# Channel mix in float32r over coefficients stored in two parts, and column transforms in full precision beside it

## The chip, the cores and the metric

The kernel runs on one core of a Trainium2 chip. The metric is the device time of one execution in microseconds (us). The engines are TensorE (PE in the profile, with its weight loads shown apart as PEld), VectorE (DVE), ScalarE (ACT), GpSimd (POOL) and SyncE (SP). [...]

## The reference

The input x has 4 images of 64 channels, each 256 x 256, in float32. Four layers follow one another. Layers 0, 1 and 3 are the same kind: per channel, a two-dimensional causal convolution with a filter that is an outer product, plus a bias times the input. Layer 2 is a Haar transform with channel mixing and soft thresholding:

```python
k = jnp.einsum('ijk,imk->ijmk', hx, hy)[0]          # layers 0, 1, 3
y = irfft2(rfft2(x) * rfft2(k) / fft_size)[..., :L, :L]
out = y + x * bias[:, None, None]
...
f1 = haar2d(x)                                       # layer 2
for i in range(2):
    f3 = f1 * v[i]
    f4 = jnp.einsum('bchw,oc->bohw', f3, conv_w[i])
    acc = acc + jnp.sign(f4) * jax.nn.relu(jnp.abs(f4) - tau[i])
y = haar2d(acc, inverse=True) + x
```

## The kernel before

**The products.** As the filters are outer products, a convolution becomes two products with Toeplitz matrices (`contract`, lines 248 and 249), in full float32: data are the stationary operand (128 x 128), a Toeplitz tile `t` of 256 or 128 columns is the moving one. A full-precision product shows as two weight loads and two matmul records. Each product's result `pa` is copied out of PSUM by ScalarE (line 262); each second result `py` gets the bias term on VectorE (line 279).

**The stages.** One image passes three stages. *Convolutions* (`convolutions`): layers 0 and 1 channel by channel, then the row part of the Haar transform on VectorE (`pairs`, `levels`, in the ring of eight tiles `sd`), then the column part on TensorE (`down`), whose result `pz` is copied by ScalarE to `co` and stored in the DRAM tensor `coef` (`away`). *Mixing* (`mixing`): 64 groups of four coefficient rows, loaded with channels on the partitions, mixed over channels on TensorE (`mix`), scaled, thresholded and added into the resident tile `z`. *Inverse* (`inverse`): channel by channel back, then layer 3. While image b is mixed and inverted, the convolutions of image b + 1 are laid between; beside the last image's mixing stand the layer-3 convolutions of a third of the channels, which had been put off to `late`.

**The column transform.** In `down` every channel is split into two float32r parts, a rounded copy (`split`, line 337, ScalarE) and the difference (`rest`, line 342, VectorE), and two products of 512 columns with the same stationary matrix `hbr` add up in PSUM. A full-precision branch with `hbt` is in the code; no channel takes it, since `in_parts` holds all of them.

**The mix.** A group's tile `f` has 128 partitions: two coefficient rows (k) by 64 channels. Slices of 128 columns are the stationary operand, and `wb`, in which the 128 x 256 matrix has the mixing weights twice on its diagonal and zeros beside, is the moving one. Four full-precision products of 256 columns make one group.

**The order.** [...] `at(time, run, unit)` collects every step with a due time in ticks, `PLACE` holds the fraction of a tick of each kind of step, and the steps are issued in the order of these times. A tick is one channel or one group. On VectorE the order in the trace departs from the due times in places, where a step's input comes later; on TensorE and ScalarE it follows them. `after` stretches the ticks of the last eight channels past `border`, the start of the inverse stage. SyncE issues nearly all loads and stores in this order, ScalarE the outputs and `late`.

**Buffers.** PSUM has four banks (`psm`) for convolutions and transforms and two double banks (`psx`) for the mix. The pool `toep` has five Toeplitz tiles; tag "in" has three tiles for loaded images; tag "f" has three, shared by the mix's loads and the inverse's `r`; tag "co" has two.

## Time and profile before

| | |
|---|---|
| time, median of 3 runs | 2973.84 us (2973.59 to 2974.6) |
| span of the profiled execution, first to last instruction | 2971.0 us |
| granted TensorE clock | 1.0 throughout |
| first convolutions, alone | until about 453 us |
| mixing stages of the four images (first to last mix product) | 453 to 858, 1088 to 1529, 1763 to 2204, 2433 to 2706 us |
| last inverse stage | from 2723 us to the end |
| moved by DMA | 649.7 MB, 219 GB/s on average |
| busy share of the 16 DMA engines | 0.76 between 30 and 420 us, 0.69 to 0.81 later |

The profiled execution's span is given; the times of the three runs are measured apart from it and lie 2.6 to 3.6 us above it. In the profile's groups, a line reads: line of the code, engine, operation, tiles written and read, shapes, count, then busy time and the mean length of one instruction, then the engine's idle time just before and what ended it. Records of matmuls overlap, since they are pipelined; the distance between their starts tells what one costs.

### The profile page before, as it was taken

Reading aid. Unit: us, or ns where it says so; the run is one execution under the profiler, and the core shown is the slowest. Engines: PE = TensorE matmul, PEld = TensorE weight load, DVE = VectorE, ACT = ScalarE, POOL = GpSimd, SP = SyncE. Lnnn points to the kernel's source line nnn. Section 1 sums busy time; section 2 is a strip of 40 time slices with the busy share of each in tenths; the row PEclk is TensorE's granted clock in tenths of the full one; section 3 lists DMA queues with packets and bytes.
Section 4 is the critical chain, followed back from the end, with each engine's and each line's share of the span. In section 5 each row is a group of like instructions: output and inputs, shape, how many; then the busy total and the mean of one; then the engine's idle time right before and its main releaser. Section 6 shows DMA issues by size and latency. Waiting matters only on the chain. (4 is left out here: it accounts for less than half of the span.)

```text
span 2971.0 us, 52173 instructions
## 1 busy us (share of the span) xinstructions
PE 2905.9 (98%) x16950; PEld 2615.2 (88%) x16950; DVE 2529.6 (85%) x4571; ACT 2183.4 (73%) x5142; POOL 0.2 (0%) x4
## 2 busy tenths in 40 slices
PE   8999999999999999999999999999999999999999
PEld 6899988888888998888888998888888998888998
DVE  5766768999988879999988878999998889998776
ACT  2333338999986768889986768999986768887554
POOL 0000000000000000000000000000000000000000
PEclk9999999999999999999999999999999999999999
DMA  5887777776667876767777876777677888777676
GB/s 156 246 235 230 225 234 213 210 208 195 210 196 238 255 222 199 210 209 208 209 220 229 255 228 199 210 211 211 206 211 231 255 245 235 234 231 220 212 211 186
DMA packets 562498, 649.74 MB, mean 219 GB/s; under 512 B 44369, under 2 KB 447412, under 8 KB 562100
## 3 DMA queue, kind: packets, MB, share of 16 engines
q1 hardware_dynamic: 482996, 562.07, 64.8%
q10 hardware_dynamic: 79232, 84.34, 8.1%
q8 instruction: 137, 2.24, 0.3%
q14 instruction: 133, 1.09, 0.1%
HBM read 426.77 MB, written 219.48 MB: 218 GB/s over the span
## 5 line engine op out<-in xcount | busy, mean ns | idle before, releaser
L248 PE MATMUL py<-t,a 128*128 128x256 f32 x3072 | 920.4, 381 | 11.7 <-ACT a L262 6.3
L262 ACT COPY a<-pa 128x512 f32<-128x512 f32 x768 | 485.8, 633 | 374.7 <-PE pa L249 338.9
L439 ACT ACTIVATE f<-px,vt 128x64 f32<-128x64 f32 x2816 | 619.9, 391 | 113.8 <-DVE f L434 113.2
L249 PEld LDWEIGHTS py<-t,a 128*128 128x128 f32 x3072 | 583.4, 190 | 79.4
L249 PE MATMUL py<-t,a 128*128 128x128 f32 x3072 | 590.0, 274 | 0.0
L248 PEld LDWEIGHTS py<-t,a 128*128 128x128 f32 x3072 | 498.4, 191 | 57.4 <-ACT a L262 18.1
L415 PE MATMUL px<-wb,f 128*128 128x256 f32 x2048 | 486.6, 380 | 6.4 <-ACT f L439 6.4
L415 PEld LDWEIGHTS px<-wb,f 128*128 128x128 f32 x2048 | 369.2, 190 | 48.3 <-ACT f L439 8.5
L248 PE MATMUL pa<-t,y 128*128 128x256 f32 x1024 | 310.0, 385 | 16.7 <-DVE y L279 15.4
L450 DVE TENSOR_TENSOR mag<-mag,vt 128x1024 f32<-128x1024 f32 x256 | 313.3, 1224 | 10.8 <-ACT mag L443 10.2
L443 ACT ACTIVATE mag<-f 128x1024 f32<-128x1024 f32 x256 | 299.8, 1171 | 20.4 <-DVE z L458 19.6
L454 DVE SCALAR_TENSOR_TENSOR mag<-mag,f 128x1024 f32<-128x1024 f32 x256 | 313.3, 1224 | 0.9
L504 ACT CAST w<-pw 128x512 fp32r<-128x512 f32 x256 | 150.3, 587 | 221.6 <-PE pw L496 208.9
L248 PE MATMUL pa<-t,x 128*128 128x256 f32 x1024 | 305.8, 380 | 1.1 <-issue 1.1
L446 ACT ACTIVATE f<-f 128x1024 f32<-128x1024 f32 x256 | 288.1, 1125 | 4.4 <-DVE y L279 1.2
L488 ACT COPY zc<-z 128x512 f32<-128x512 f32 x256 | 282.5, 1104 | 10.9 <-DVE z L289 6.3
L342 DVE TENSOR_TENSOR sp<-sd,sp 128x512 fp32r<-128x512 f32 x256 | 176.5, 689 | 105.0 <-ACT sp L337 103.6
L248 PE MATMUL pa<-t,u 128*128 128x256 f32 x772 | 231.0, 381 | 10.2 <-issue 9.5
L519 DVE SCALAR_TENSOR_TENSOR t<-r,pu 128x512 f32<-128x512 f32 x256 | 175.5, 685 | 65.6 <-PE pu L511 65.0
L279 DVE SCALAR_TENSOR_TENSOR y<-x,bsb,py 128x512 f32<-128x512 f32 x256 | 190.8, 745 | 39.3 <-PE py L249 39.2
L279 DVE SCALAR_TENSOR_TENSOR y<-y,bsb,py 128x512 f32<-128x512 f32 x256 | 190.3, 744 | 38.0 <-PE py L249 37.8
L249 PEld LDWEIGHTS pa<-t,y 128*128 128x128 f32 x1024 | 194.5, 190 | 26.4
(67 smaller groups left out, 4470.8 us busy)
## 6 DMA issues: line engine op xcount, KB each, us to landing
t<-pad SPq DMA_DIRECT2D x768, 256.0 KB, 3.9
x<-in_x SPq DMA_DIRECT2D x256, 256.0 KB, 3.6
keep<-sd SPq DMA_DIRECT2D x256, 256.0 KB, 2.9
coef<-co SPq DMA_DIRECT2D x256, 256.0 KB, 3.1
f<-coef SPq DMA_DIRECT2D x256, 256.0 KB, 3.3
r<-keep SPq DMA_DIRECT2D x256, 256.0 KB, 3.3
out_y<-y ACTq DMA_DIRECT2D x256, 256.0 KB, 4.0
late<-u ACTq DMA_DIRECT2D x63, 256.0 KB, 3.0
```

The source lines that it names most:

```text
L248: nc.tensor.matmul(ps[:, m, :], src[:, 0, m * P : (m + 1) * P], t[:, ::-1], start=True, stop=False)
L249: nc.tensor.matmul(ps[:, m, P:], src[:, 1, m * P : (m + 1) * P], t[:, : P - 1 : -1], start=False, stop=True)
L262: nc.scalar.copy(a, s["p" + new])
L279: nc.vector.scalar_tensor_tensor(y, s[res], bsb[:, layer, c : c + 1], s["p" + new], ALU.mult, ALU.add)
L342: nc.vector.tensor_tensor(w[:, 1], t, w[:, 0].bitcast(F32), ALU.subtract)
L415: nc.tensor.matmul(ps[:, h, q, :], f[:, q, h * P : (h + 1) * P], wb.rearrange("p r n -> p (r n)"), start=True, stop=True,)
L439: nc.scalar.mul(f4[:, j], px[:, j], scale(g, 0)[:, j : j + 1])
L443: nc.scalar.activation(mag, st[g]["f4"], AF.Abs)
L446: nc.scalar.activation(st[g]["f4"], st[g]["f4"], AF.Sign)
L450: nc.vector.tensor_sub(mag, mag, over(g, 1, 16))
L454: nc.vector.scalar_tensor_tensor(mag, mag, 0.0, st[g]["f4"], ALU.max, ALU.mult)
L488: nc.scalar.copy(a, z[:, :, :, c].rearrange("p h (i k) -> p h k i", k=2))
```

## The change

The diff below does the following.

- `coef` gets another layout and twice the size: a float32r rounding of each coefficient (`hi`) and the float32 difference to it (`lo`), each channel's two coefficient rows side by side. `away` writes the rounded copy. A new step `low`, due 0.316 ticks later, subtracts on VectorE and stores the difference; until then the PSUM bank stays in use.
- A group's tile `f` now has the two parts by 64 channels on its 128 partitions and holds 512 KB instead of 256. It has two buffers instead of three, is typed float32r, and is loaded from GpSimd's queue.
- `wb` holds the mixing weights, the same on both halves of the partitions, in two float32r parts. `mix` makes 16 float32r products of 128 columns a group: for each of the eight output slices one with the small part of the weights and one with the large, added up in PSUM.
- `down` takes the full-precision product for channels that fall due before `border`, in other words beside a mixing stage; the others keep the two parts. `split` and `rest` fall away with it. The first image has no border and keeps all its parts.
- The inverse's `r` moves to tag "in".

```diff
+    "low": 1.05,
...
-    wb = const.tile([P, 2, P], F32, name="wb")
+    wb = const.tile([P, 2, P], F32R, name="wb")
...
-    coef = [dram.tile([2, C, P, S], F32, name=f"coef{b}") for b in range(B)]
+    coef = [dram.tile([2, C, P, 2, S], F32, name=f"coef{b}") for b in range(B)]
...
-        nc.vector.memset(wb, 0.0)
         for r in range(2):
-            nc.sync.dma_start(wb[r * C : (r + 1) * C, r, :], wmix)
+            nc.sync.dma_start(mixw[r * C : (r + 1) * C, :], wmix)
+        nc.scalar.copy(wb[:, 0], mixw)
+        nc.vector.tensor_tensor(wb[:, 1], mixw, wb[:, 0].bitcast(F32), ALU.subtract)
...
         def away(c):
-            t = io.tile([P, 2, S], F32, name=f"co_{b}_{c}", tag="co", bufs=BUFS["co"])
-            nc.scalar.copy(t, parts.pop(("ps", c)))
-            nc.sync.dma_start(coef[b][:, c].rearrange("k p w -> p k w"), t)
+            t = parts["hi", c] = mx.tile([P, 2, S], F32R, name=f"hi_{b}_{c}", tag="hi")
+            nc.scalar.copy(t, parts["ps", c])
+            nc.sync.dma_start(coef[b][0, c].rearrange("p k w -> p (k w)"), t.bitcast(F32).rearrange("p k w -> p (k w)"))
+
+        def low(c):
+            t = mx.tile([P, 2, S], F32R, name=f"lo_{b}_{c}", tag="lo", bufs=1)
+            nc.vector.tensor_tensor(t, parts.pop(("ps", c)), parts.pop(("hi", c)).bitcast(F32), ALU.subtract)
+            nc.sync.dma_start(coef[b][1, c].rearrange("p k w -> p (k w)"), t.bitcast(F32).rearrange("p k w -> p (k w)"))
...
-                if c in in_parts:
+                if border is None or end + 4 + j >= border:
+                    in_parts.add(c)
                     at(after(end + 3 + j, n) + PLACE["split"], split, c)
                     at(after(end + 3 + j, n) + PLACE["rest"], rest, c)
...
+                at(after(end + 4 + j, n) + PLACE["low"], low, c)
...
-            f = mx.tile([P, 2, S], F32, name=f"f_{b}_{g}", tag="f", bufs=3)
-            nc.sync.dma_start(f, coef[b].rearrange("k c p w -> (k c) p w")[:, 2 * g : 2 * g + 2])
+            f = mx.tile([P, 2, 2, S], F32R, name=f"f_{b}_{g}", tag="f", bufs=2)
+            nc.gpsimd.dma_start(f, coef[b].rearrange("l c p k w -> (l c) p k w")[:, 2 * g : 2 * g + 2])
...
-            for q in range(2):
-                for h in range(2):
-                    nc.tensor.matmul(
-                        ps[:, h, q, :],
-                        f[:, q, h * P : (h + 1) * P],
-                        wb.rearrange("p r n -> p (r n)"),
-                        start=True,
-                        stop=True,
-                    )
+            for h in range(2):
+                for q in range(2):
+                    for r in range(2):
+                        for i in (1, 0):
+                            nc.tensor.matmul(
+                                ps[:, h, q, r * P : (r + 1) * P],
+                                f[:, q, r, h * P : (h + 1) * P],
+                                wb[:, i],
+                                start=(i == 1),
+                                stop=(i == 0),
+                            )
...
-            r = mx.tile([P, 2, 2, P], F32, name=f"r_{b}_{c}", tag="f", bufs=3)
+            r = io.tile([P, 2, 2, P], F32, name=f"r_{b}_{c}", tag="in", bufs=3)
...
-    nc = _bacc.Bacc("TRN2", target_bir_lowering=False, num_devices=1)
+    nc = _bacc.Bacc("TRN2", target_bir_lowering=False, num_devices=1, dynamic_dma_scratch_size=2048)
```

More of the change, by code (lines that the diff above doesn't have):

```diff
@@ L206, in constants @@
     def constants():
-        signs = part(P)
+        signs, mixw = part(P), part(P)
         nc.sync.dma_start(hbt, haar[0])
@@ L297, in at, with convolutions @@
         events.append((time, len(events), run, unit))
-    def convolutions(b, ticks, in_parts=(), border=None):
+    def convolutions(b, ticks, border=None):
         st = {}
+        in_parts = set()
         def after(tick, n):
@@ L582, in conv_seq_kernel @@
     groups = S // 4
-    ready = convolutions(0, range(C), in_parts=range(C))
+    ready = convolutions(0, range(C))
     ahead = C
@@ L589, in conv_seq_kernel @@
         if b + 1 < B:
-            ready = convolutions(b + 1, spread(ahead, end + 2), in_parts=range(C), border=end)
+            ready = convolutions(b + 1, spread(ahead, end + 2), border=end)
         else:
```

## The prediction

> **What bounds the kernel now.** I read the page's top first: how full each engine is.

> ```profile
> span 2971.0 us, 52173 instructions
> PE 2905.9 (98%) x16950; PEld 2615.2 (88%) x16950; DVE 2529.6 (85%) x4571; ACT 2183.4 (73%) x5142; POOL 0.2 (0%) x4
> ```

> TensorE (PE) is idle for 2971.0 - 2905.9 = 65 us, 14 of them in the first 30 us. An average can hide a stage with another limit, so next the windows by stage: the four mixing stages (columns: length, PE, weight loads, VectorE, ScalarE, GpSimd, clock, DMA share, GB/s).

> ```profile
> 453.00:858.00 405.00, 398.49 (x2179) 350.37 (x2179) 381.86 (x671) 396.73 (x1203) 0.00 (x0) 1.00 0.69 205
> 1088.00:1529.00 441.00, 435.14 (x2440) 391.42 (x2440) 409.39 (x717) 388.21 (x1094) 0.00 (x0) 1.00 0.71 208
> 1763.00:2204.00 441.00, 435.70 (x2441) 391.87 (x2440) 409.67 (x718) 388.70 (x1094) 0.00 (x0) 1.00 0.70 208
> 2433.00:2706.00 273.00, 267.62 (x1454) 239.72 (x1454) 266.13 (x314) 235.87 (x556) 0.00 (x0) 1.00 0.80 234
> ```

> PE is 98% busy in each. In the first, ScalarE is as full (397 of 405); in the last, VectorE (266 of 273). So added PE time lengthens a stage almost one for one, while removed PE time soon meets another engine. The groups that the change touches:

> ```profile
> L415 PE MATMUL px<-wb,f 128*128 128x256 f32 x2048 | 486.6, 380 | 6.4 <-ACT f L439 6.4
> L349 PE MATMUL pz<-sp,hbr 128*128 128x512 f32 x512 | 182.3, 436 | 1.2 <-DVE y L279 0.6 <-DVE sp L342 0.4
> L337 ACT CAST sp<-sd 128x512 fp32r<-128x512 f32 x256 | 184.0, 719 | 3.9 <-DVE sd L328 3.9
> L342 DVE TENSOR_TENSOR sp<-sd,sp 128x512 fp32r<-128x512 f32 x256 | 176.5, 689 | 105.0 <-ACT sp L337 103.6
> L505 DVE TENSOR_TENSOR w<-pw,w 128x512 fp32r<-128x512 f32 x256 | 175.3, 685 | 2.3 <-ACT w L504 2.3
> ```

> Means of pipelined matmuls overlap, so PE prices are distances between starts in the timeline:

> ```profile
> 803.39 0.60 PE L248 MATMUL py<-t,a 128*128 128x256 f32 x2
> 803.83 0.39 PE L249 MATMUL py<-t,a 128*128 128x128 f32 x2
> ```
> ```profile
> 1003.30 0.38 PE L495 MATMUL pw<-hrow,zc 128*128 128x128 f32 x2
> 1003.51 0.27 PE L496 MATMUL pw<-hrow,zc 128*128 128x128 f32 x1
> 1003.62 0.39 PE L495 MATMUL pw<-hrow,zc 128*128 128x128 f32 x2
> ```
> ```profile
> 464.16 0.19 PEld L349 LDWEIGHTS pz<-sp,hbr 128*128 128x128 f32 x1 [0.35 <-DVE sp L342]
> 464.27 0.42 PEld L248 LDWEIGHTS py<-t,a 128*128 128x128 f32 x2
> 464.50 0.59 PE L248 MATMUL py<-t,a 128*128 128x256 f32 x2
> ```

> First fence: a full-precision product over 256 columns (two records) takes 0.43 us, so 0.216 a record. Second: three records of 128 columns take 0.32-0.33 us, about 0.11 each, even the single-record transpose L496. Third, a float32r product whose load had to wait: the next load can start 0.11 after its load, the next product 0.34 after it. So its weight load takes 0.11, and its 512 columns take 0.23. The load is not shorter in float32r.

> [...]

> **The change, part by part.**

> 1. *Mix.* Before: 4 full-precision products of 256 columns a group = 8 x 0.216 = 1.73 us. After: 16 float32r products of 128 columns, each with a weight load of its own (L349 uses one stationary operand twice in a row and still has 512 loads for 512 products, so a repeated one isn't skipped). Streaming 128 columns should take 0.23 / 4 = 0.06, the load 0.11; loads follow one another at 0.11 in the L495/L496 chain. The load sets the pace: 16 x 0.111 = 1.78. Over 256 groups: +0.05 x 256 = **+12 us**. No narrow float32r product is in the trace: bounds are 0.058 (load hidden) and 0.216 [...], which is -205 and +442 us. I take 0.111.

> 2. *Column transforms in full precision.* From the ticks, 54 + 53 + 53 = 160 of 256 channels fall due before the border and get one full-precision product of 512 columns: twice 0.43 = 0.86. The float32r pair takes 0.47 (L249 x2 at 1002.61, L495 at 1003.30: 0.69 less 0.22 for the L249 pair). So +0.39 x 160 = **+63 us** of PE, 21 in each of the first three mixing stages. These channels lose the copy L337 (-0.72 x 160 = -115 us of ScalarE) and the difference L342 (-110 us of VectorE); both hide beside PE.

> 3. *Storing two parts.* The copy out of PSUM stays. New is "low", a subtraction like L505: 0.685 x 256 = +175 us of VectorE, net +65. In mixing, 54 come for 54 gone; in the first convolutions (265 of 390 us busy) 44 us are added. All beside PE. Its wait: it needs ScalarE's copy. Behind it stand add, the y1 sum and the next group's scaling, for which ScalarE's row scaling waits (113 us in all already). But L342 waits for ScalarE alike (103.6 us in 104 waits) and is gone there; VectorE's order in the trace follows readiness, not only due times, so I expect "low" about where L342 was: 0. If it stands ahead of add and y1 sum, the round scaled, ScalarE (2.98 + 0.46 + 0.6), low 0.61, add 0.6, y1 sum 0.66, pairs 0.67, shrink 1.13, scaled 0.3 comes to 8.0 us in the first stage, where PE wants 6.5; with 0.8 channels a group up to +70 us, some +100 over all. The PSUM bank is held some 1.5 us longer; its next user is the fourth bank request after it, some 4 us on: 0. "lo" has one buffer: its transfer (3.1 us for coef) ends well within a tick of 6 to 7 us; where ticks last 3.2 us, about two channels a batch wait some 1 us: 0 to +5.

> 4. *Transfers.* SP loses the group load and gains one store a channel; its stores wait for "low", with toeplitz and x loads behind, some 1.5 us a tick of slack that those loads have (landing 3.6 to 3.9 against 0.93 tick, 5.7 us). The load of 512 KB leaves from GpSimd, whose queue holds nothing else; a buffer comes free when group g-2 is mixed, so it has two groups less one mix: 2 x 4.25 - 1.8 = 6.7 us in the last stage, 11 and more elsewhere. The landing:

> ```profile
> coef<-co SPq DMA_DIRECT2D x256, 256.0 KB, 3.1
> f<-coef SPq DMA_DIRECT2D x256, 256.0 KB, 3.3
> ```

> 3.3 us at 256 KB; [...] It fits. Load on the engines: 134 MB on 650; in the last stage +0.5 us in 4.25, 0.80 to about 0.92 busy; in the first convolutions from 0.76 to 0.87. I allow +5 for slower toeplitz loads.

> 5. *Rest.* r moves from three buffers to three shared with x; only where a last x load falls between the first r loads does one wait, 0.1 us. Splitting the weights (two instructions of 0.3 us) lies beside the first convolutions. ScalarE's 39 us less in each mixing stage may take back over half of the 17.7 us that PE is idle in the three (6.5 + 5.9 + 5.3 in the windows): -10.

> Sum: 2971.0 + 12 + 63 + 5 - 10 + 3 (lo, rest) = 3044 of span. The profiled execution's span lies 2.8 us under the median 2973.84; kept, that gives **3047 us**.

> **The rivals.**
> - *Faster: narrow products hide their load.* [...] At 0.058, 2885, VectorE stopping it. The point is 0.0925 a product: (1.73 - 16t) x 256 = 63. [...] Against: the 0.11 load.
> - *Narrow float32r at the full-precision price.* 0.216 a product: 3.46 a mix, 3047 - 12 + 442 = 3477. Nothing in the trace excludes it[...].
> - *Load and stream don't quite overlap.* A float32r stream takes 0.017 more for its 512 column steps than the 0.216 record; added to each load: 0.128 x 16 = 2.05, about 3117.
> - *The group load is late.* From 6.7 us in the last stage: at 8 us, 1.3 x 64 = +83, 3130.
> - *"low" ahead of its input*, above: up to 3145.
> - *Nothing moves*: t at 0.0925 by chance.

> **How the numbers follow.** Likeliest 59% (3025 to 3075); imperfect overlap 7%, late load 8%, low's wait 7% (3075 to 3150); full price 9%; faster 8%; within 0.2% 2%. Measurement of this kernel tells 0.2% from no change. The range 3010 to 3150 leaves out the full price, the faster case and the unchanged one, 19%. Slower sums to 0.90.

> **What would show it.** Right: mixes start to next product 1.75 to 1.80 us, weight loads 18,998; the transform product 0.86 with 160 + 192 products; mixing stages some 24 us longer, the last some 3; PE still at 98%. Wrong: [...]PE waiting for the group load (step 4), VectorE waiting for the copy with PE idle behind (step 3).

## The result and the profile after

The changed kernel takes 3508.32 us (median of 4 runs, 3503.24 to 3512.85) against 2974.22 us before (4 runs, 2973.59 to 2975.87): 1.179 times as long, 95% interval 1.1777 to 1.181. The prediction was 3047 us in a range of 3010 to 3150. The direction was right; the size missed by 461 us.

The top of the changed kernel's page (busy time, share of the span, instructions):

```profile
span 3503.0 us, 56614 instructions
PE 3139.4 (90%) x18998; PEld 2783.9 (79%) x18998; DVE 2611.7 (75%) x4667; ACT 2110.6 (60%) x4983; POOL 135.6 (4%) x260
```

The weight loads number 18,998, as predicted, but TensorE now idles 3503.0 - 3139.4 = 364 us, where it idled 65. VectorE and ScalarE are emptier too. No engine is full any more. The windows of the four mixing stages (columns as in the prediction):

```profile
473.00:1031.00 558.00, 464.39 (x2687) 402.73 (x2687) 394.78 (x681) 382.40 (x1154) 32.76 (x62) 0.92 0.65 200
1264.00:1831.00 567.00, 496.26 (x2985) 431.46 (x2984) 418.51 (x723) 362.88 (x1047) 32.76 (x62) 0.97 0.71 214
2070.00:2639.00 569.00, 497.32 (x2981) 432.59 (x2980) 418.38 (x724) 363.15 (x1048) 32.77 (x62) 0.97 0.71 213
2874.00:3235.00 361.00, 299.36 (x1965) 276.06 (x1963) 278.91 (x319) 241.14 (x563) 32.76 (x62) 0.94 0.77 221
```

The stages grew from 405, 441, 441 and 273 us to 558, 567, 569 and 361: 495 us of the 532. In each, TensorE idles 62 to 94 us, and its granted clock is 0.92 to 0.97. Even the last stage grew by 88 us, though it holds no column transforms. The transfers are no busier than in the first convolutions before (0.77 between 30 and 450 us). The groups of instructions that the change touches:

```profile
L427 PE MATMUL px<-wb,f 128*128 128x128 f32 x4096 | 530.3, 284 | 3.4 <-ACT mag L455 1.0 <-DMA f<-coef 1.0 <-ACT f L451 0.8
...
L368 DVE TENSOR_TENSOR lo<-pz,hi 128x512 fp32r<-128x512 f32 x256 | 176.0, 688 | 200.6 <-ACT hi L363 163.0 <-DMA coef<-lo 30.7 <-ACT sp L340 6.8
L356 PE MATMUL pz<-sd,hbt 128*128 128x512 f32 x320 | 166.6, 603 | 0.0
...
L352 PE MATMUL pz<-sp,hbr 128*128 128x512 f32 x192 | 68.5, 438 | 0.0
L345 DVE TENSOR_TENSOR sp<-sd,sp 128x512 fp32r<-128x512 f32 x96 | 65.5, 683 | 3.2 <-ACT sp L340 3.0
```

The mix products (L427) wait for almost nothing: 3.4 us in all. 320 records make 160 full-precision transforms (L356), and 192 float32r products remain (L352). Durations between starts, from TensorE's timeline:

```profile
1506.12 1.98 PE L427 MATMUL px<-wb,f 128*128 128x128 f32 x16
1507.93 0.65 PE L250 MATMUL py<-t,a 128*128 128x256 f32 x2
...
1510.61 1.02 PE L356 MATMUL pz<-sd,hbt 128*128 128x512 f32 x2
1511.46 0.59 PE L250 MATMUL py<-t,a 128*128 128x256 f32 x2
```

A mix takes 1.81 us to the next product's start (0.113 a product; 0.111 was predicted), a transform 0.85 (0.86 was predicted). As a record's start shifts with its neighbours (the 256-column product behind this mix has 0.49 us to the next start, 1507.93 to 1508.42, the one behind that 0.43, 1508.64 to 1509.07), a safer measure runs from the start of the product ahead to that of the second product behind. Its medians are 2.38 us around a mix before and 2.44 after (+0.06, where +0.05 was predicted), and 1.12 around a transform in two parts and 1.51 around one in full precision (+0.39, as predicted). The landing times, from the list of DMA issues:

```profile
f<-coef POOLq DMA_DIRECT2D x256, 512.0 KB, 4.6
...
coef<-hi SPq DMA_DIRECT2D x256, 256.0 KB, 3.4
coef<-lo SPq DMA_DIRECT2D x256, 256.0 KB, 2.9
```

4.6 us for the doubled load, where 256 KB took 3.3 before, is below the 6.7 us that step 4 gives it in the last stage. `low` itself takes 0.688 us (0.685 was predicted). So the prices of the products and of the subtraction were met, the mix products wait 1.0 us in all for the load, and most of the time lies elsewhere. The list of waits says where (engine and line, what it waited for: total us, times, longest):

```profile
ACT f L451 <- DVE f L446: 664.9, 250, 7.6
...
DVE mag L462 <- ACT mag L455: 305.2, 136, 3.4
...
PEld pa L250 <- DVE y L281: 196.2, 147, 5.3
DVE lo L368 <- ACT hi L363: 163.0, 93, 3.3
PE pa L250 <- DVE y L281: 152.7, 133, 5.1
```

To read this, the steps of a group: VectorE scales its part of the mix's result (`scaled`) and ScalarE the other rows (row scaling); ScalarE takes the absolute value (Abs) and the sign; VectorE subtracts the threshold (`shrink`), cuts at zero and puts the sign back (`signed`), and adds the result into `z` (`add`). ScalarE's row scaling (L451) waits for VectorE's `scaled` (L446) 665 us; before, the same pair cost 113. VectorE's `shrink` (L462) waits for ScalarE's Abs (L455) 305 us; before 10. Each waits for the other, and TensorE waits for VectorE's y sums (L281). A stretch of VectorE's timeline before (L450 is shrink, L434 scaled, L454 signed, L458 add):

```profile
1297.20 0.42 DVE L434 TENSOR_TENSOR f<-px,vt 128x256 f32<-128x256 f32 x1
...
1303.01 1.22 DVE L450 TENSOR_TENSOR mag<-mag,vt 128x1024 f32<-128x1024 f32 x1
1304.14 0.42 DVE L434 TENSOR_TENSOR f<-px,vt 128x256 f32<-128x256 f32 x1
1304.48 1.22 DVE L454 SCALAR_TENSOR_TENSOR mag<-mag,f 128x1024 f32<-128x1024 f32 x1
1305.61 0.75 DVE L279 SCALAR_TENSOR_TENSOR y<-x,bsb,py 128x512 f32<-128x512 f32 x1
1306.27 0.69 DVE L458 TENSOR_TENSOR z<-mag 128x512 f32<-128x512 f32 x1
```

And after (L462 shrink, L466 signed, L470 add, L446 scaled):

```profile
1515.93 0.69 DVE L368 TENSOR_TENSOR lo<-pz,hi 128x512 fp32r<-128x512 f32 x1 [1.94 <-ACT hi L363]
1516.54 0.74 DVE L281 SCALAR_TENSOR_TENSOR y<-y,bsb,py 128x512 f32<-128x512 f32 x1
1517.19 1.22 DVE L462 TENSOR_TENSOR mag<-mag,vt 128x1024 f32<-128x1024 f32 x1
...
1519.00 1.22 DVE L466 SCALAR_TENSOR_TENSOR mag<-mag,f 128x1024 f32<-128x1024 f32 x1
1520.25 0.69 DVE L470 TENSOR_TENSOR z<-mag 128x512 f32<-128x512 f32 x1
1520.86 0.42 DVE L446 TENSOR_TENSOR f<-px,vt 128x256 f32<-128x256 f32 x1
```

ScalarE's timeline over the same stretch:

```profile
1512.38 2.56 ACT L451 ACTIVATE f<-px,vt 128x64 f32<-128x64 f32 x12 [2.95 <-DVE f L446]
...
1515.69 1.17 ACT L455 ACTIVATE mag<-f 128x1024 f32<-128x1024 f32 x1
...
1521.32 2.56 ACT L451 ACTIVATE f<-px,vt 128x64 f32<-128x64 f32 x12 [2.89 <-DVE f L446]
```

Before, `scaled` of the next group stands between shrink and signed of this one, so ScalarE scales the next group while VectorE finishes this one. After, it stands behind shrink, signed and add. Row scaling, Abs, shrink, signed, add, scaled and the next row scaling then follow one another (in this tick `low` and the y1 sum stand ahead of shrink as well), and a group takes 1521.32 - 1512.38 = 8.94 us instead of 1304.14 - 1297.20 = 6.94 (the distance of two `scaled` before). VectorE's trace keeps the order of its stream: in the first three images `scaled` runs behind signed 63 times of 63, as in the table below. Here L446 runs behind L470, at 1520.86, while ScalarE stands 2.89 us for it.

Nothing in the diff moves `scaled`: its due time and those of the steps beside it are unchanged, and by them `scaled` of the next group comes ahead of shrink (1.583 ticks against 1.777 in the first three images). So the due times alone don't make the order. They feed a scheduler that writes each engine's stream when the kernel is compiled; the experiments below change that order by rules of order alone, and the traces follow them. Counted in VectorE's stream, for the 63 neighbouring groups of each image, `scaled` of g + 1 stands ahead of shrink of g / between shrink and signed / behind signed:

```
                                    image 1     image 2     image 3     image 4
before                              45 18  0     8 50  5     8 50  5    58  4  1
after                                0  0 63     0  0 63     0  0 63     0 27 36
product alone (narrow_only)          0 14 49     0  0 63     0  0 63     0 27 36
transforms alone (down_only)        15 28 20     8  8 47     8  8 47    58  4  1
second copy alone (low_only)        57  6  0    31 27  5    31 27  5    58  4  1
after, 8 products of 256 columns    61  2  0    28 34  1    28 34  1    61  2  0
```

### The profile page after: what moved, and what is told of

Same layout as the page of the kernel before. It is cut to its first block, busy times and chain, and to the rows that moved or that the text cites. A ratio compares the mean times of both kernels' runs of the same rounds, so it can differ in the third digit from the quotient of the medians.

```text
span 3503.0 us, 56614 instructions
## 1 busy us (share of the span) xinstructions
PE 3139.4 (90%) x18998; PEld 2783.9 (79%) x18998; DVE 2611.7 (75%) x4667; ACT 2110.6 (60%) x4983; POOL 135.6 (4%) x260
## 5 line engine op out<-in xcount | busy, mean ns | idle before, releaser
L250 PE MATMUL py<-t,a 128*128 128x256 f32 x3072 | 957.8, 394 | 130.7 <-ACT a L264 126.3
L451 ACT ACTIVATE f<-px,vt 128x64 f32<-128x64 f32 x2816 | 607.0, 345 | 672.8 <-DVE f L446 664.9
L251 PE MATMUL py<-t,a 128*128 128x128 f32 x3072 | 603.5, 279 | 0.0
L462 DVE TENSOR_TENSOR mag<-mag,vt 128x1024 f32<-128x1024 f32 x256 | 313.2, 1223 | 307.5 <-ACT mag L455 305.2
L427 PE MATMUL px<-wb,f 128*128 128x128 f32 x4096 | 530.3, 284 | 3.4 <-ACT mag L455 1.0
L427 PEld LDWEIGHTS px<-wb,f 128*128 128x128 f32 x4096 | 500.7, 199 | 4.8 <-ACT f L451 2.8
L250 PE MATMUL pa<-t,y 128*128 128x256 f32 x1024 | 332.5, 407 | 157.1 <-DVE y L281 151.7
L250 PE MATMUL pa<-t,x 128*128 128x256 f32 x1024 | 327.4, 403 | 43.8 <-DVE lo L368 35.9
L368 DVE TENSOR_TENSOR lo<-pz,hi 128x512 fp32r<-128x512 f32 x256 | 176.0, 688 | 200.6 <-ACT hi L363 163.0
L466 DVE SCALAR_TENSOR_TENSOR mag<-mag,f 128x1024 f32<-128x1024 f32 x256 | 312.7, 1221 | 12.7 <-ACT f L458 7.2
L250 PEld LDWEIGHTS pa<-t,y 128*128 128x128 f32 x1024 | 158.9, 195 | 201.3 <-DVE y L281 194.4
L455 ACT ACTIVATE mag<-f 128x1024 f32<-128x1024 f32 x256 | 292.0, 1141 | 1.7
L458 ACT ACTIVATE f<-f 128x1024 f32<-128x1024 f32 x256 | 281.8, 1101 | 4.3
L407 POOL DMA_DIRECT2D f<-coef x256 | 135.4, 529 | 3087.9 <-PE px L427 2055.5
L330 DVE TENSOR_TENSOR sd<-sd 128x512 f32<-128x512 f32 (+6 forms) x448 | 164.6, 367 | 107.0 <-DMA keep<-sd 57.9
## 6 DMA issues: line engine op xcount, KB each, us to landing
t<-pad SPq DMA_DIRECT2D x768, 256.0 KB, 4.1
x<-in_x SPq DMA_DIRECT2D x256, 256.0 KB, 3.7
keep<-sd SPq DMA_DIRECT2D x256, 256.0 KB, 3.5
coef<-hi SPq DMA_DIRECT2D x256, 256.0 KB, 3.4
coef<-lo SPq DMA_DIRECT2D x256, 256.0 KB, 2.9
r<-keep SPq DMA_DIRECT2D x256, 256.0 KB, 3.5
out_y<-y ACTq DMA_DIRECT2D x256, 256.0 KB, 3.7
```

Source lines behind the costliest of these rows:

```text
L250: nc.tensor.matmul(ps[:, m, :], src[:, 0, m * P : (m + 1) * P], t[:, ::-1], start=True, stop=False)
L251: nc.tensor.matmul(ps[:, m, P:], src[:, 1, m * P : (m + 1) * P], t[:, : P - 1 : -1], start=False, stop=True)
L368: nc.vector.tensor_tensor(t, parts.pop(("ps", c)), parts.pop(("hi", c)).bitcast(F32), ALU.subtract)
L427: nc.tensor.matmul(ps[:, h, q, r * P : (r + 1) * P], f[:, q, r, h * P : (h + 1) * P], wb[:, i], start=(i == 1), stop=(i == 0),)
L451: nc.scalar.mul(f4[:, j], px[:, j], scale(g, 0)[:, j : j + 1])
L455: nc.scalar.activation(mag, st[g]["f4"], AF.Abs)
```

## The experiments

The theory: the work costs about what was predicted, and most of the excess comes from the order on VectorE. The rivals: the narrow products, the new storage or the second copy cost more than their durations show. Ratios are to the kernel before on the same chip, with 95% intervals.

### The order rule on the changed kernel (after_pinned)

```diff
-            nc.vector.tensor_tensor(
+            st["scaled", g] = nc.vector.tensor_tensor(
...
-            nc.vector.tensor_sub(mag, mag, over(g, 1, 16))
+            with tc.issue_after(st["scaled", g + 1].ins):
+                nc.vector.tensor_sub(mag, mag, over(g, 1, 16))
```

> The changed kernel with one ordering rule added and nothing else: on VectorE the subtraction that shrinks group g may not stand ahead of the scaling of group g + 1 (issue order only, no wait). Order theory (the compiler's instruction order on VectorE lost the look-ahead of the scaling, and ScalarE and VectorE take turns): most of the loss goes, 3030 to 3080 us, ScalarE's wait for the scaling falls from 665 us to under 200, PE busy over 97%. Theory of the new step's wait (the subtraction of the low part waits for ScalarE's copy and holds VectorE and the PSUM bank): 3400 or more, since that wait stays. Theory of the doubled group load from GpSimd: 3400 or more.

Measured: 3295.63 us, 1.1079 (1.1063 to 1.1096). 213 us come back, so order is a cause, but the expectation was missed by over 200, and the rivals' 3400 as well. The rule fixes one pair of steps only: ScalarE still waits 446.5 us for `scaled`, and the scheduler arranged the other steps anew around it.

### Each part alone

Product alone, with a load of 256 KB from GpSimd; coefficients and weights are rounded and not split, and each product is made twice, so the sum isn't the reference's:

```diff
-                    nc.tensor.matmul(
-                        ps[:, h, q, :],
-                        f[:, q, h * P : (h + 1) * P],
-                        wb.rearrange("p r n -> p (r n)"),
+                    for r in range(2):
+                        for i in (1, 0):
+                            nc.tensor.matmul(
+                                ps[:, h, q, r * P : (r + 1) * P],
+                                f[:, q, h * P : (h + 1) * P],
+                                wb[:, r],
```

> The kernel before, with the mix alone as 16 float32r products of 128 columns a group (group load from GpSimd, 256 KB, coefficients and weights only rounded and not split, each slice computed twice). No low part, no full-precision transforms, three buffers. Order theory: the order on VectorE changes with the narrow products alone, so most of the loss is here, 3200 to 3450 us, with a PE product still at 0.11 us. Theory of the new step's wait: 2986 (only +12 us of PE). Theory of the load's size: 2986.

Measured: 3431.99 us, 1.1538 (1.1521 to 1.1556). Product alone brings 458 us of the loss, without the second copy, the 512 KB load or the full-precision transforms. ScalarE waits 560.8 us for `scaled`. The expectation held, but the rival could still say that narrow products are slow. With the order rule on top:

> The same kernel with narrow products alone, plus the ordering rule. Order theory: 2975 to 3000 us, the 12 us of PE that 16 weight loads of 0.111 cost over 8 records of 0.216. Were narrow products slow in themselves: as slow as without the rule.

Measured: 3166.91 us, 1.0642 (1.0624 to 1.066). Missed again, by 167 us: TensorE now waits 122.5 us for y sums (L281) that stand late on VectorE (3.19 us at 1387.69, for example, in a tick that holds Haar levels), and VectorE's `scaled` 70.0 us for the mix itself. A rule on one pair is too little to test the theory.

Transforms alone (the diff's change to `in_parts`, nothing else), without and with the rule:

> The kernel before with full-precision column transforms beside the mixing stages alone. PE price of the prediction: +63 us, 3037, a product of 0.86 us. Order theory: the compiler's order keeps less of the look-ahead here too (the scaling of group g + 1 stands behind the last use of group g in 47 of 63 groups of the middle images), so more than that, 3040 to 3120.

> The same kernel with full-precision transforms alone, plus the rule that the shrinking of group g stands behind the scaling of group g + 1 on VectorE. Order theory: 3030 to 3050 us. If the order doesn't matter here: as without the rule.

Measured: 3051.46 us, 1.0252 (1.0236 to 1.0268), and with the rule 3013.32 us, 1.0125 (1.0109 to 1.0141). The first lies in its range, the second undercut it. Here, too, the table shows a worsened order (47 of 63 behind signed in images 2 and 3), which could be read from the compiled streams before the run.

Second copy alone, with the lost group buffer:

```diff
+        def low(c):
+            t = mx.tile([P, 2, S], F32, name=f"lo_{b}_{c}", tag="lo", bufs=1)
+            nc.vector.tensor_tensor(t, parts.pop(("ps", c)), parts.pop(("hi", c)), ALU.subtract)
+            nc.sync.dma_start(spare[b, c].rearrange("p k w -> p (k w)"), t.rearrange("p k w -> p (k w)"))
...
-            f = mx.tile([P, 2, S], F32, name=f"f_{b}_{g}", tag="f", bufs=3)
+            f = mx.tile([P, 2, S], F32, name=f"f_{b}_{g}", tag="f", bufs=2)
```

> The kernel before, with the second copy alone: each transformed channel's PSUM bank is subtracted from and stored a second time (to a DRAM tensor that nobody reads), two group buffers, r in the image's tag. The mix stays in full precision. Order theory: the look-ahead of the scaling stays, so 2970 to 3010 us. Theory of the new step's wait: the bulk of the 530 us is here, 3200 or more.

Measured: 3032.28 us, 1.0194 (1.0179 to 1.0209), +58 us, 22 above the range of the order theory and far below the 3200 of the rival. By the count of the table its look-ahead is kept, but its order isn't that of the kernel before in all else. 23 us of the 58 fall in the first convolutions, where no mix runs. Steps 3 and 4 had 0 to 5 and 5 for all this.

### The whole order of two engines

As a rule on one pair let the scheduler shift the rest, the next runs fix the whole stream of VectorE and ScalarE. The streams are taken from another kernel with the same instructions, and entered as order alone:

```diff
+    for a, b in zip(order[:-1], order[1:]):
+        info = mybir.DependencyInfo(mybir.DependencyClass.NoSync, mybir.DependencyReason.DATA)
+        tc.add_manual_dep(ins[b], ins[a].name, info, reason="issue order")
```

The first donors are the kernels with products of 256 columns in place of the narrow ones (the table's last line, and the like for product alone).

> The changed kernel, every instruction and wait of it kept, with VectorE and ScalarE issuing in the order that the compiler writes for a twin whose mix has 8 float32r products of 256 columns in place of 16 of 128 (both have the same instructions on these engines; the twin keeps the scaling one group ahead). Order theory: the loss falls to its parts on PE and the second copy, 12 + 63 + 58 (the second copy alone measured 3032 against 2974) = 3107 us, between 3060 and 3140, with the granted clock back near 1. If narrow products, the doubled load or the storage held the chip up in themselves: 3250 or more.

Measured: 3135.79 us, 1.0545 (1.0524 to 1.0565). 373 us come back with not one instruction taken out, and the time lies in the range. The last mixing stage still takes 333 us.

> The kernel before with narrow float32r products alone (unsplit, each slice twice), VectorE and ScalarE issuing in the order that the compiler writes for a twin with 4 products of 256 columns. Order theory: 2975 to 3000 us, the 12 us of PE being all that is left of 458. If the first rule (3167 with it) had already taken all that order explains: 3150 or more.

Measured: 3085.35 us, 1.0363 (1.0343 to 1.0382): better by 347 us than the compiler's order, but missed. 60 of the 111 us lie in the last mixing stage (332 against 272), where the donor's order was made for another mix. So the next run gives product alone the order of the kernel before (from the 401st instruction of each engine on, at some 280 us of VectorE and 490 us of ScalarE):

> Product alone (16 float32r products of 128 columns a group, on unsplit coefficients, each slice used twice, so the sum over the parts isn't the reference's; one 256 KB load a group from GpSimd), with VectorE and ScalarE in exactly the order of the kernel before. By the order theory only step 1's 256 x 0.05 = 12 us remain: 2980 to 3000, no image's mixing stage more than 6 us over that of the kernel before. If narrow products cost something that the distance between starts doesn't show (the first three images of the run with the order of the wide products stood 22, 14 and 14 us over): 3020 to 3040. If the load from GpSimd is late in the last stage: that stage 20 us or more over 272.

Measured: 2984.16 us, 1.0039 (1.0023 to 1.0054): +12.3 us, where step 1 said +12. Of the 458 us of product alone, 446 were order. The parts agree less well than the sum: the first mixing stage grew by 7 us, above the 6 that were allowed, the other three by 0 to 3. ScalarE's wait for `scaled` in the list of waits; product alone in the compiler's order:

```profile
ACT f L443 <- DVE f L438: 560.8, 250, 5.2
```

and in the order of the kernel before:

```profile
ACT f L443 <- DVE f L438: 125.9, 137, 4.6
```

The same cure for the whole change, with a donor of its own for the last image:

> The whole change; VectorE and ScalarE issue in the order of the 256-column variant for the first three images and, from the last image's mixing on, in the order that the compiler writes when the group's products are the four full-precision ones. By the order theory the last mixing stage falls from 333 to 270 to 280, the first three stay (426, 468, 466), and the whole comes to 3070 to 3090: 2974 + 12 (mix) + 77 (transforms, as run alone) + 58 (second copy, as run alone) less what the three share. If the last stage waits for the 512 KB load of 4.6 us: it stays above 310, the whole near 3130.

Measured: 3090.07 us, 1.0397 (1.0383 to 1.0411). Its windows of the mixing stages:

```profile
473.00:896.00 423.00, 417.84 (x2693) 371.87 (x2691) 375.00 (x671) 377.64 (x1155) 32.76 (x62) 1.00 0.87 264
1124.00:1592.00 468.00, 463.87 (x2986) 414.71 (x2985) 406.58 (x720) 368.92 (x1049) 32.77 (x62) 1.00 0.85 259
1827.00:2295.00 468.00, 463.35 (x2980) 414.02 (x2980) 406.32 (x720) 369.04 (x1048) 32.77 (x62) 1.00 0.85 259
2528.00:2820.00 292.00, 276.70 (x1963) 260.55 (x1963) 271.40 (x316) 236.90 (x556) 32.77 (x62) 0.99 0.93 274
```

and its waits:

```profile
ACT f L451 <- DVE f L446: 203.8, 160, 4.2
...
DVE lo L368 <- ACT hi L363: 24.3, 38, 2.0
...
PE px L427 <- DMA f<-coef: 11.2, 11, 1.9
```

In the first three stages TensorE idles 4 to 5 us each and the clock is back at 1. Only the last, at a DMA share of 0.93, now waits for group loads: 11.2 us on the products themselves. The last stage came to 292 where 270 to 280 was expected; the whole stands at the upper end of its range. TensorE's products follow one another in the same sequence in this trace and in that of the changed kernel, so the difference is the order of VectorE and ScalarE. Which of the two counts for how much was not tried apart.

### Is it the width?

```diff
-                        for i in (1, 0):
-                            nc.tensor.matmul(
-                                ps[:, h, q, r * P : (r + 1) * P],
-                                f[:, q, r, h * P : (h + 1) * P],
-                                wb[:, i],
+                        nc.tensor.matmul(
+                            ps[:, h, q, :],
+                            f[:, q, r, h * P : (h + 1) * P],
+                            wb.rearrange("p r n -> p (r n)"),
```

> The whole change but the shape of the product: 8 float32r products of 256 columns a group over the same coefficients, loads and stores (the two weight parts are used as one 256-column operand, so the sum isn't the reference's), order left to the compiler. Order theory: the compiler's VectorE order looks ahead again, so although the same storage, group load and second copy are there, no stage shows ScalarE waiting for scaled as in the changed kernel (665 us there, under 200 here); the mix takes about 8 x 0.12 = 0.95, 0.8 us less a group than the 16, and VectorE bounds what that gives: 2940 to 3060. If the new storage or load makes the stalls: above 3300.

Measured: 3046.69 us, 1.0247 (1.0233 to 1.0261), in the order that the compiler writes by itself, with the new storage, the GpSimd loads, the second copy and the transforms all in place. ScalarE waits 163.9 us for `scaled`. So the form of the product (16 of 128 columns instead of 8 of 256) turns the order, and the storage doesn't. Whether it is the width or the number of the products was not tried apart. Why the scheduler puts narrow products so stays open: no run showed what it takes them to cost. These 8 products also take TensorE less time, so 3047 is no measure of the order alone. By the safer measure above, less the 0.22 and 0.43 us of the neighbours, a product of 256 columns costs 0.119 us here and one of 128 columns 0.112 in the changed kernel: half the columns save next to nothing, as step 1 had it.

### What the second copy pays for

> The kernel before with two group buffers and the second subtraction (PSUM less ScalarE's copy) on VectorE, but no second store. If the added subtraction makes the 58 us of the run with both (its time on VectorE, or the PSUM bank that it holds longer): 3015 to 3035. If the added store does: 2972 to 2990.

> As the run with the second subtraction and store, but the subtraction reads ScalarE's copy twice instead of the PSUM bank (so the second copy stored is zero), and the bank comes free at the copy as before; VectorE's time, the wait for ScalarE and both stores stay. If the bank held longer makes the loss: 2980 to 3000, and the 22 us of the first convolutions gone. If it is VectorE's time or the stores: 3020 to 3035.

> As the run with the second subtraction and store, but without the subtraction: ScalarE's copy is stored twice, two group buffers. If the stores or the lost group buffer make the loss: 3010 to 3030. If the subtraction does: 2972 to 2985.

Measured: subtraction without its store 2995.07 us (1.0072, 1.0054 to 1.009); both, but with the PSUM bank released at the copy, 3029.56 us (1.0185, 1.0163 to 1.0207); store without subtraction 3001.53 us (1.0096, 1.008 to 1.0112). The first and the last fit neither of their ranges; the second fits the one that acquits the bank.

All of them have two group buffers, so the 22 us of the first and the 28 us of the last, to the kernel before on their chip (2973.21), each hold the lost buffer. But the first and the run with both have the same buffers and, in their traces, all but the same order on TensorE, ScalarE and VectorE (some twenty of VectorE's 4827 instructions stand elsewhere). They differ by the second store: 3032.28 - 2995.07 = 37 us, the larger part of the 58. 22 us of the 37 lie in the first convolutions (476.1 us against 454.4). There VectorE waits 23.1 us, in 10 waits, for the store before it to leave the one `lo` buffer; whether that makes the 22 isn't shown. The other 22 us are the subtraction, the lost buffer and another order together. The released bank changes 3 us (3032.28 - 3029.56), inside the scatter of either, and VectorE's order changed with it. In the run with the store alone VectorE's order in the mixing is that of the kernel before (the counts of the table's first line); 11 of its 28 us lie in the first convolutions (464.3 us against 453.3), the rest in the mixing stages of images 2 and 3. The lost buffer alone was not run.

### The order rule on the kernel before

> The kernel before with the order rule alone (VectorE issues shrink of group g only behind scaled of group g+1); nothing else differs. If the rule is neutral for a kernel whose order was good: 2968 to 2980. If it takes back part of the 17 us that TensorE idles in the first three mixing stages, as the run with the rule and the full-precision transforms suggests (its stages grew 11 to 13 us where 21 of products were added): 2945 to 2968. If the rule harms by itself, as the product-only run with the rule leaves possible (it stood 192 us over the kernel before): above 3000.

Measured: 2965.14 us (9 runs), 0.9976 (0.9966 to 0.9985), in the second range. It is a little faster than the kernel before, and the fastest kernel with the reference's whole computation here. The wait of TensorE's `pa` products for y sums falls from 15.4 to 9.5 us; a gain of 7 us fits the little idle time that was left. So the rule does no harm by itself.

## Why the prediction was wrong

The step that failed is one that the sum didn't contain: that all other instructions keep their places. Step 3 saw the danger for the new subtraction alone and dismissed it with "VectorE's order in the trace follows readiness, not only due times". The trace of one kernel can't show that: where order and readiness agree, nothing tells which made the other. The term for a new order stood at nothing, without a reason of its own. In the changed kernel VectorE waits in its written order for inputs that come late (305.2 us at shrink and 163.0 us at `low`, for ScalarE). Order, of VectorE and ScalarE together, explains 3508.32 - 3090.07 = 418 us of the 461.

The remaining 43 us are sizes:

- **Step 1, mix, +12.** Right: +12.3 with the order kept, and 0.06 x 256 = 15 by the timeline. The load sets the pace: in the changed kernel's trace the weight loads of a mix follow one another at 0.112 (median), the products at 0.112 to 0.113. That the sum came within half a microsecond is luck, as its stages show.
- **Step 2, transforms, +63, with 10 taken back by step 5.** Mechanism right. With the order rule in both, 3013.32 - 2965.14 = 48 us (by the ratios 1.0125 and 0.9976, 44), against 53. The price was right (+0.39).
- **Step 3, subtraction, 0 to +5.** Too small: 22 us, with the lost buffer and a shifted order in it. That a subtraction "beside PE" is free isn't upheld. For the PSUM bank, put at nothing, no cost clear of the scatter was found. The one `lo` buffer cost VectorE 30.7 us of waiting in the changed kernel, perhaps a part of the store's price below.
- **Step 4, transfers, +5.** The load landed in 4.6 us, within the 6.7 of the last stage, and with the good order the last stage is 0.93 busy (0.92 predicted). But that stage is 19 us longer than before, not 3: TensorE idles 15 us in it, 11 of them for group loads, so "It fits", an estimate of the author's, doesn't quite hold at that share. And one more store a channel, for which the loads were said to have slack, costs 37 us; most of it shows in the first convolutions, which end at 473 us instead of 453.

With measured sizes, 12 for the mix, 44 to 48 for the transforms and 58 for the second copy give 114 to 118; the change in good order costs 118 (3090.07 - 2971.85). As the parts were measured in different orders and leave out the doubled load, this close a fit is in part luck. The first three stages grew by 18, 27 and 28 us, where 24 each was said.

The rivals: "full price" named 3477, near the measured time, by a mechanism that the first timeline excludes, since a narrow product takes 0.113 and not 0.216. "`low` ahead of its input" had the right kind of wait (163 us on L368, 24 once the order is good), and nearly the round of waits, at 8.0 us a group in the first stage, where 558 / 64 = 8.7 was measured; but it took only `low` as movable and so ended at 3145. Product alone, without `low`, loses 458 us all the same. "The group load is late" came true in small, 11 us where 83 were named. The faster case fell with the 0.113. "PE still at 98%" was the sign to watch: it fell to 90% with the prices of the products met, which leaves order and waits.

## What to carry to other kernels

When a scheduler orders the engines' streams as the kernel is compiled, a change on one engine can reorder another that the diff doesn't touch. Compare the order of each engine's stream before and after, which needs no chip, before adding up durations. When prices are met and yet all engines idle more, look for two engines that wait for each other, and test by giving one kernel the other's order, whole and not one pair of it.

## What the runs showed of the hardware

```profile
610.20:613.60 3.40, 3.40 (x24) 2.66 (x22) 2.98 (x4) 1.09 (x4) 0.00 (x0) 1.00 0.98 265
613.60:617.00 3.40, 0.96 (x9) 0.82 (x9) 1.82 (x3) 3.40 (x16) 0.53 (x1) 1.00 0.69 196
617.00:620.40 3.40, 3.40 (x14) 3.02 (x15) 3.23 (x9) 2.31 (x3) 0.00 (x0) 0.65 0.45 163
```

At 618.03 us, within the last of these windows, the clock halves for 3.41 us; in the 3.41 us ahead TensorE was busy for 1.17. The same two products ahead of that stretch and in it:

```profile
609.62 0.60 PE L250 MATMUL pa<-t,x 128*128 128x256 f32 x2
610.05 0.38 PE L251 MATMUL pa<-t,x 128*128 128x128 f32 x2
...
618.49 1.06 PE L250 MATMUL pa<-t,x 128*128 128x256 f32 x2
619.34 0.64 PE L251 MATMUL pa<-t,x 128*128 128x128 f32 x2
```

The 256-column product takes 0.43 us at full clock and 0.85 at half. In the whole trace the half clock comes in stretches of 3.41 us and multiples, 199 us within the span, against 0.1 in the trace of the kernel before. All 45 begin on one grid of 3.41 us. Of the grid's windows at full clock in which TensorE was busy less than 40%, 29 of 33 were followed by half clock (the other four begin in the first 14 us); of those between 40 and 70%, 16 of 94; of those above 70%, none of 841. So a window partly busy was often enough, as in the example (1.17 of 3.41 us). TensorE was busy in 190 of the 199 us, so about 95 us of its work were lost, an estimate. That is a large part of why its busy time, 3139 us, fell to 3001 in the good order with the same products, where the mean granted clock is 0.997 (0.972 in the changed kernel). As far as it held anything up, this loss is part of the 418 us of order.
